# First layers of 18 groups of experts' tokens by seven products of half blocks, with weight sums made on GpSimd

## The chip, the core and the metric

The kernel runs on one core of a Trainium2 chip. The metric is the device time of one launch in microseconds: the median of three runs before is 1558.56 us (1558.34 to 1558.69). A core has five engines that matter here, each with a queue of its own that it works off strictly in order: PE (matrix products; PEld is its loading of weights), DVE (elementwise work, reads PSUM and SBUF), ACT (activations and copies, reads PSUM and SBUF), POOL (GpSimd: elementwise work on SBUF, and the indirect DMAs) and SP (which issues the other DMAs). Engines wait for each other through semaphores. [...]

## What is computed

One layer: a graph aggregation over a 4096 x 4096 matrix, an attention block, and a mixture of eight experts, of which each token takes two. The change is in the experts. All is float32.

```python
for e in range(NE):                       # NE = 8, HID = 682, C = 256
    hh = jax.nn.silu(flat @ w1[e].T) * (flat @ w3[e].T)
    out = out + weights[:, e:e + 1] * (hh @ w2[e].T)
return x + out.reshape(Bx, Tx, Cx)
```

`flat @ w1.T` and `flat @ w3.T` are the first layers, `hh @ w2.T` the second.

## The kernel before

The graph and the attention take the first 1043 us. Then the tokens, sorted by expert into `lists` in DRAM, are worked off in groups of one expert each: whole groups of 256 tokens and small groups of 128. `TURNS` lists them in order; k is the place in it, 0 to 41. Places 0 to 8 are whole, 9 to 36 mix 11 whole ones (10, 12, 15, 17, 20, 22, 25, 28, 30, 33, 35) with 17 small ones, 37 to 41 are whole. Nothing is rescheduled by a planner: each engine gets its instructions in the order in which the Python code issues them, and semaphores are put between.

For each k the loop runs, in this order: `hidden(k)`, the first layers with the activation, ending with the transposes and scaling of the next group's tokens (`prepare(k + 1)`: transposes `tx` on PE, two scalings L1383 on ACT); `load13(k + 5)`, the weights of both first layers; `combine(k - 1)`, the second layer of the group before, its weighting by the router, and an indirect DMA that adds each half of 128 tokens into DRAM (L1548 on POOL, after a short memset of `gap`); then `load_rows(k + 4)` and `load2(k + 4)`. Five buffers each hold w13, w2 and rows, `w13s[k % 5]` and so on.

`hidden` of a whole group: the hidden units are five blocks of 128 (`NF = 5`) and a rest of 42 units, whose w1 and w3 columns share one block. For each of these 11 blocks and both halves of C, one product of 128 x 128 weights with 128 x 256 tokens (L1476). They go to PSUM tiles of one or two banks from three pools (`p_sc0`, `p_sc1`, `p_sc2`, six banks together, shared with the attention's scores and accumulators `y_first` and `y_second`). ACT takes silu (L1482), DVE multiplies by the other product into `hT` (L1483).

Second layers of the 19 whole groups in `SEVEN` (k = 4 to 39) are already done in seven products of half blocks (Strassen's scheme in Winograd's form): `split(k)` makes four sums of quarters of hT and four of w2 on DVE (L1412 to L1419), `seven_products` does seven products of three blocks each (L1440), with 128 tokens or channels to a product, into two banks (`ye_y`, `ye_ms`), and adds them up with one copy on ACT (L1447) and seven adds on DVE (L1448 to L1454). ACT then weights both halves into y (L1539).

Of the kernel before, what the change touches and what calls it, by code (L numbers as in the profile page):

```python
# [9 lines left out]
F32 = mybir.dt.float32  # L10
# [5 lines left out]
PSUM = bass.MemoryType.PSUM  # L16
# [49 lines left out]
def fast_kernel(  # L66
# [596 lines left out]
    with (  # L663
# [1 line left out]
        tc.tile_pool(name="eg", bufs=1) as eg,  # L665
        tc.tile_pool(name="ex", bufs=2) as ex,
        tc.tile_pool(name="ax", bufs=2) as ax,
        tc.tile_pool(name="a_sc0", bufs=1, space=PSUM) as p_sc0,
        tc.tile_pool(name="a_sc1", bufs=2, space=PSUM) as p_sc1,
        tc.tile_pool(name="a_sc2", bufs=1, space=PSUM) as p_sc2,  # L670
        tc.tile_pool(name="a_y", bufs=1, space=PSUM) as p_y,
        tc.tile_pool(name="a_ms", bufs=1, space=PSUM) as p_ms,
    ):

        HALF = GR // P
        pt_all = sp.tile([P, 9 * 1024], F32, name="pt_all")
# [25 lines left out]
            given_back.update(keys)  # L702
            ring[:] = [r for r in ring if homes.get(id(r)) not in given_back]

        p_sc = cycle((p_sc0, p_sc2, p_sc1))
        p_sa = cycle((p_sc0, p_sc2))
        y_banks = [
            pool.tile([P, 512], F32, tag=tag, name=name) for pool, tag, name in (
# [681 lines left out]


        SEVEN = [k for k in range(4, NM - 2) if TURNS[k] < NW]
        parts_of = {}

        def split(k, hT):


            w2_sb = w2s[k % 5]
            m = {}
            for c in range(2):  # L1400
                chunks = hT.rearrange("p (j c) i -> p c j i", c=2)[:, c]
                weights = w2_sb.rearrange("p (j c) o -> p c j o", c=2)[:, c]
                for h in range(2):
                    m[f"A{h + 1}{c + 1}"] = chunks[:, :, h * P : (h + 1) * P]
                    m[f"G{c + 1}{h + 1}"] = weights[:, :, h * P : (h + 1) * P]
            first = k % 2 * 3
            for n, s in enumerate(("S1", "S2", "S4")):
                m[s] = kT[first + n][:, 0 : 3 * P].rearrange("p (j i) -> p j i", j=3)
            for n, s in enumerate(("T1", "T2", "T4")):
                m[s] = vv[first + n][:, 0:3, :]  # L1410
            m["S3"], m["T3"] = m["A21"], m["G12"]
            nc.vector.tensor_add(m["S1"], m["A21"], m["A22"])  # L1412
            nc.vector.tensor_sub(m["S2"], m["S1"], m["A11"])
            nc.vector.tensor_sub(m["S4"], m["A12"], m["S2"])
            nc.vector.tensor_sub(m["S3"], m["A11"], m["A21"])
            nc.vector.tensor_sub(m["T1"], m["G12"], m["G11"])
            nc.vector.tensor_sub(m["T3"], m["G22"], m["G12"])
            nc.vector.tensor_sub(m["T2"], m["G22"], m["T1"])
            nc.vector.tensor_sub(m["T4"], m["T2"], m["G21"])  # L1419
            parts_of[k] = m  # L1420
# [36 lines left out]
        def hidden(k, step=None, behind=None):  # L1457
# [4 lines left out]
            free_bank = k >= SEVEN[0]  # L1462

            for q in range(0, NF + 1, 2):
                pool = next(p_sc)
                if pool is p_sc1:
                    ps = [
                        pool.tile([P, 2, GR], F32, tag="sc", name=f"h_{i}_{q}_{m}")[:, :, 0:n]
                        for m in range(2)
                    ]  # L1470
                else:
                    ps = pool.tile([P, 2, 2, GR], F32, tag="sc", name=f"h_{i}_{q}")
                    ps = [ps[:, m, :, 0:n] for m in range(2)]
                for m in range(2 * q, min(2 * q + 4, 2 * NF + 1)):
                    for c in range(2):
                        nc.tensor.matmul(  # L1476
                            ps[m % 2][:, m // 2 - q, :], w13_sb[:, c, m * P : (m + 1) * P],
                            xT[:, c, :], start=(c == 0), stop=(c == 1),
                        )
                both = 2 if q + 1 < NF else 1  # L1480
                si = ax.tile([P, 2, n], F32, tag="rden", name=f"si_{i}_{q}")
                nc.scalar.activation(si[:, 0:both, :], ps[0][:, 0:both, :], AF.Silu)  # L1482
                nc.vector.tensor_mul(  # L1483
                    hT[:, q : q + both, :], si[:, 0:both, :], ps[1][:, 0:both, :]
                )
                if q == 0 and behind is not None and not free_bank:
                    prepare(behind)
                if step and q < NF - 1:
                    step()
# [4 lines left out]
            )  # L1494
            if behind is not None and free_bank:
                prepare(behind, p_ms, "ms")
            hidden_of[i] = hT
            if k in SEVEN:
                split(k, hT)
# [146 lines left out]
        def step():  # L1646
            for f in next(rest, []):
                f()

        load13(2)  # L1650
        load2(2)
        load13(3)
# [2 lines left out]
        for k in range(NM):  # L1655
            if k == NM - 1:


                between = iter([lambda: None, lambda: combine(k - 1)])
            hidden(  # L1660
                k, step if k < NM - 1 else lambda: next(between)(),
                k + 1 if k + 1 < NM else None,
            )
            step()
            if k + 5 < NM:
                load13(k + 5)
            if 0 < k < NM - 1:
                combine(k - 1)
                step()
            if k == NM - LAST:  # L1670
                nc.sync.dma_start(out, acc_dram[0:N, :])
            if k + 4 < NM:
                load_rows(k + 4)
            if k + 4 < NM:
                load2(k + 4)
        combine(NM - 1)
    kv_scope.close()
    return lists

# [736 lines left out]
```

## Time and profile before

The profile is one execution of 1558.78 us, of which the span from first to last instruction is 1557.0 us.

| | before |
|---|---|
| median of three runs | 1558.56 us |
| profiled execution, its span | 1558.78 us, 1557.0 us |
| PE busy | 1541.9 us |
| DVE, ACT, POOL busy | 1045.4, 488.1, 655.0 us |
| stretch of the experts 1100 to 1500 us: PE busy | 400.0 us of 400 |
| the same: DVE, ACT, POOL busy | 197.4, 103.6, 94.2 us |
| granted PE clock in that stretch | 1.00 |

How to read it: rows of the timeline give the start, the length, engine, line, operation, output and inputs of one instruction or of a merged run of equal ones, then in brackets how long the engine sat idle before it and what released it. In rows by form, the two numbers after the bar are the group's busy time in us and the mean of one in ns. Each float32 product shows as two records on PE, so the 22 products of a whole group's first layers are 44 rows.

### The profile page before, as it was taken

The numbers are of one execution on the slowest core, as the hardware profiler recorded it, in microseconds if no ns is written. First come the engines' busy times: TensorE is split into PE (matmuls) and PEld (weight loads), VectorE is DVE, ScalarE is ACT, GpSimd is POOL, SyncE is SP. The second block draws the span as 40 slices with busy tenths as digits, with TensorE's granted clock in tenths as the row PEclk, the third lists the DMA queues.
The fourth block names the chain that finished last, engine by engine and source line by source line (L and its number), as shares of the span: only waits on it lengthen the run. The fifth ranks groups of instructions, "written<-read, shape, count | busy, mean of one in ns | idle before, by whom it ended". The sixth has DMA issues, their size and how long they took to land.

```text
span 1557.0 us, 27444 instructions
## 1 busy us (share of the span) xinstructions
PE 1541.9 (99%) x10692; PEld 1133.8 (73%) x10692; DVE 1045.4 (67%) x2137; ACT 488.1 (31%) x884; POOL 655.0 (42%) x725
## 2 busy tenths in 40 slices
PE   8999999999999999999999999999999999999997
PEld 7888888888888643444444444358899999999996
DVE  7966677766766677779879878785565453544462
ACT  1101010010010356555665655652122222222221
POOL 3446557565565323364564553442422212122213
PEclk9999999999999999999999999999999999999999
DMA  6344444443444000011011011048677778777772
GB/s 236 129 129 146 139 139 135 139 139 136 139 136 142 32 1 16 29 36 51 29 57 33 29 39 37 22 184 314 192 229 207 228 249 264 232 242 246 237 232 29
DMA packets 68507, 209.34 MB, mean 134 GB/s; under 512 B 17488, under 2 KB 45520, under 8 KB 54736
## 3 DMA queue, kind: packets, MB, share of 16 engines
q1 hardware_dynamic: 55104, 189.50, 35.5%
q0 software_dynamic: 12720, 17.47, 5.8%
q8 instruction: 86, 1.41, 0.4%
q10 hardware_dynamic: 544, 0.52, 0.1%
q14 instruction: 53, 0.43, 0.1%
HBM read 184.48 MB, written 27.13 MB: 136 GB/s over the span
## 4 chain that ended last, share of the span: by engine, by line
PE 96%; DVE 2%; DMA 0%; POOL 0%; issue 0%; ACT 0%; SPq 0%; POOLq 0%; DVEq 0%; ACTq 0%
PE acc L493 25%; PE h L1476 21%; PE sc L757 14%; PE y_first L799 5%; PE y_second L799 5%; PE ye_y L1528 4%; PE y_third L799 4%; PE ye_y L1440 3%; PE ye_ms L1440 2%; PE pq L194 2%; PE ph L545 2%; PE pf L464 1%; PE po L876 1%; PE tx L1377 1%; PE trq L229 1%; PE tr L376 1%
## 5 line engine op out<-in xcount | busy, mean ns | idle before, releaser
L757 PE MATMUL sc<-qT_all,kT 64*64 64x512 f32 (+3 forms) x2304 | 282.0, 557 | 1.0 <-ACT pt_all L765 0.5
L493 PE MATMUL acc<-a,g 128*128 128x256 f32 x1024 | 245.9, 380 | 0.0
L1548 POOL DMA_INDIRECT acc_dram<-y,late x57 | 89.8, 1575 | 334.9 <-DVE y L1543 185.5
L493 PEld LDWEIGHTS acc<-a,g 128*128 128x128 f32 x1024 | 193.0, 190 | 31.6 <-DVE vv L511 1.2
L757 PEld LDWEIGHTS sc<-qT_all,kT 64*64 64x64 f32 x2304 | 91.2, 133 | 130.1 <-issue 108.2
L1483 DVE TENSOR_TENSOR late<-si,h 128x256 f32<-128x256 f32 (+2 forms) x126 | 62.7, 506 | 183.0 <-ACT si L1482 180.2
L765 ACT ACTIVATE pt_all<-sc 128x1024 f32<-128x1024 f32 (+3 forms) x157 | 149.0, 956 | 95.7 <-PE sc L757 95.1
L448 POOL TENSOR_TENSOR all_s<-all_s,more_sums 128x512 f32<-128x512 f32 x72 | 106.4, 1491 | 106.0 <-DVE more_sums L440 106.0
L1476 PE MATMUL h<-late,qT_all 128*128 128x256 f32 (+1 forms) x792 | 147.2, 345 | 0.0
L1482 ACT ACTIVATE si<-h 128x256 f32<-128x256 f32 (+2 forms) x126 | 57.0, 453 | 276.6 <-PE h L1476 269.4
L1476 PEld LDWEIGHTS h<-late,qT_all 128*128 128x128 f32 x792 | 130.1, 191 | 15.2 <-ACT late L1383 0.8
L493 PE MATMUL acc<-more_sums,g 128*128 128x256 f32 x512 | 126.2, 379 | 0.0
L785 DVE TENSOR_TENSOR late<-late,pt_all 128x1024 f32<-128x1024 f32 (+3 forms) x92 | 107.7, 1171 | 23.0 <-ACT pt_all L765 9.6
L1476 PE MATMUL h<-late,pt_all 128*128 128x128 f32 (+1 forms) x704 | 113.5, 321 | 0.0
L1476 PEld LDWEIGHTS h<-late,pt_all 128*128 128x128 f32 x704 | 103.5, 191 | 8.0
L493 PEld LDWEIGHTS acc<-more_sums,g 128*128 128x128 f32 x512 | 97.2, 190 | 14.8
L799 PE MATMUL y_second<-pt_all,vv 64*64 64x512 f32 (+3 forms) x440 | 105.0, 555 | 0.0
L799 PE MATMUL y_first<-pt_all,vv 64*64 64x512 f32 (+3 forms) x440 | 104.3, 553 | 0.0
L1035 POOL DMA_INDIRECT lists<-row,slots x64 | 90.2, 1410 | 18.0 <-issue 15.3
L799 PE MATMUL y_third<-pt_all,vv 64*64 64x512 f32 (+3 forms) x376 | 89.8, 557 | 0.0
L378 ACT COPY qT_all<-tr 128x512 f32<-128x512 f32 x30 | 16.2, 589 | 210.5 <-PE tr L376 210.4
L1476 PE MATMUL h<-late,res_all 128*128 128x256 f32 (+1 forms) x352 | 68.3, 353 | 0.0
(394 smaller groups left out, 2997.4 us busy)
## 6 DMA issues: line engine op xcount, KB each, us to landing
a<-in_adj_dram SPq DMA_DIRECT2D x64, 1024.0 KB
qT_all<-in_w_dram SPq DMA_DIRECT2D x18, 1408.0 KB
pt_all<-in_w_dram SPq DMA_DIRECT2D x16, 1408.0 KB
res_all<-in_w_dram SPq DMA_DIRECT2D x17, 768.0 KB
pt_all<-in_w_dram SPq DMA_DIRECT2D x16, 768.0 KB
res_all<-in_w_dram SPq DMA_DIRECT2D x8, 1408.0 KB
qT_all<-in_w_dram SPq DMA_DIRECT2D x9, 768.0 KB
late<-lists SPq DMA_DIRECT2D x25, 265.0 KB
```

Of the source, the lines that this page charges most:

```text
L448: nc.gpsimd.tensor_add(all_s[:, i], all_s[:, i], sums_at[n % 2][k])
L493: nc.tensor.matmul(acc[bank][:, at, :], g[jb][:, right, k, :], m[left][:, k, :], start=(jb == 0 and k == 0 and at == 0), stop=(jb == NB - ...
L757: nc.tensor.matmul(ps[k * HP : (k + 1) * HP, j, :w], kT[sb][hd, i * P + k * HP : i * P + (k + 1) * HP], qT[b][hd, p, off:], start=True, st ...
L765: nc.scalar.activation(pt[:, :, :w], ps[:, :, :w], AF.Exp, scale=HD ** -0.5)
L785: nc.vector.tensor_add(sums[b, p][:, :, off:], before[:, :, off:], pt[:, :, : 512 - off])
L799: nc.tensor.matmul(accs[b, p][k][hd, off:], vv[sb][some, i, hd], pt[some, j, : 512 - off], start=(s == order_of(b)[0]), stop=(s == order_o ...
L1035: put = nc.gpsimd.indirect_dma_start(out=lists[:, :], out_offset=bass.IndirectOffsetOnAxis(ap=chosen[b][:, k, t, :], axis=0), in_=flats[b] ...
L1440: nc.tensor.matmul(p[number], m[left][:, j, :], m[right][:, j, :], start=(n % 4 == 0 and j == 0), stop=(j == 2), skip_group_check=True,)
L1476: nc.tensor.matmul(ps[m % 2][:, m // 2 - q, :], w13_sb[:, c, m * P : (m + 1) * P], xT[:, c, :], start=(c == 0), stop=(c == 1),)
L1483: nc.vector.tensor_mul(hT[:, q : q + both, :], si[:, 0:both, :], ps[1][:, 0:both, :])
L1528: nc.tensor.matmul(ps[h if last else 0][:, h, :], hT[:, q, cols], w2_sb[:, q, :], start=(q == 0), stop=(q == NF),)
L1548: put = nc.gpsimd.indirect_dma_start(out=(acc_dram if k < NM - LAST else out)[:, :], out_offset=at, in_=y[:, h, :], in_offset=None, comput ...
```

## The change

The 18 groups `SPLIT13 = SEVEN[1:]` (k = 5, 6, 7, 8, the 11 mixed ones, 37, 38, 39) get their first layers in seven products for eight. With A the weights (rows: w1 or w3; columns: half of C) and B the tokens (rows: half of C; columns: half of the 256 tokens), the sums of weights are S1 = A21 + A22, S2 = S1 - A11, S4 = A12 - S2, S3 = A11 - A21, each 128 x 640, and of tokens T1 to T4, each 128 x 128. Each of the seven products is done for five blocks of 128 units with 128 tokens. The 42 remaining units keep their two products with 256 tokens.

- `sums13(k)` makes S1 to S4 on GpSimd; the loop calls it with k + 2 after `hidden` of k and ahead of `combine(k - 1)`. S3 is written over A21.
- `sums2(k)` makes two of the second layer's weight sums (T1, T3, 128 x 384) on GpSimd, a group ahead after `combine(k - 1)`; `split` leaves these two out on DVE.
- `sums_x(k)` makes the four sums of tokens on DVE after the tokens are prepared.
- `hidden_seven(k)` replaces `hidden(k)`. Blocks 0 to 3 are part `one`, block 4 is part `two`; each part has three banks, A, D and B. Products are added up in a bank: ACT copies a bank's value out, PE then adds the next product on top.
- The three pools of scores are closed after the attention, and a new pool `e_h` of six single banks serves all first layers, those of `hidden` too.

```diff
+        def sums13(k):
...
+            nc.gpsimd.tensor_add(m["S1"], m["A21"], m["A22"])
+            nc.gpsimd.tensor_sub(m["S2"], m["S1"], m["A11"])
+            nc.gpsimd.tensor_sub(m["S4"], m["A12"], m["S2"])
+            nc.gpsimd.tensor_sub(m["S3"], m["A11"], m["A21"])
+        def sums_x(k):
...
+            nc.vector.tensor_sub(m["T1"], m["B12"], m["B11"])
+            nc.vector.tensor_sub(m["T2"], m["B22"], m["T1"])
+            nc.vector.tensor_sub(m["T3"], m["B22"], m["B12"])
+            nc.vector.tensor_sub(m["T4"], m["B21"], m["T2"])
+        def hidden_seven(k, step, behind):
...
+            def product(q, bank, left, right, first=False):
+                for n, c in enumerate(q.chunks):
+                    nc.tensor.matmul(
+                        bank[:, n, :], m[left][:, c, :], m[right],
+                        start=first and n == 0, stop=True, skip_group_check=True,
+                    )
+            def copied(dst, q, bank):
+                nc.scalar.copy(dst, bank[:, 0 : len(q.chunks), :])
+            def added(dst, q, bank):
+                nc.vector.tensor_add(dst, dst, bank[:, 0 : len(q.chunks), :])
+            def begun(q):
+                product(q, q.A, "A11", "B11", True)
+                copied(q.s1, q, q.A)
+                product(q, q.D, "S1", "T1", True)
+                copied(q.s5, q, q.D)
+                product(q, q.B, "A12", "B21", True)
+            def second(q):
+                product(q, q.A, "S2", "T2")
+                copied(q.u2, q, q.A)
+                product(q, q.D, "S4", "B22")
+            def joined(q):
+                added(q.s1, q, q.B)
+                added(q.u2, q, q.D)
+                nc.scalar.activation(q.pair, q.pair, AF.Silu)
+            def third(q):
+                product(q, q.A, "S3", "T3")
+                copied(q.u3, q, q.A)
+                nc.vector.tensor_add(q.u3, q.u3, q.s5)
+            def last(q):
+                product(q, q.A, "A22", "T4")
+                nc.vector.tensor_mul(hT[:, q.rows, P:GR], q.u2, q.u3)
+                nc.vector.tensor_mul(
+                    hT[:, q.rows, 0:P], q.s1, q.A[:, 0 : len(q.chunks), :]
+                )
+            begun(one)
+            second(one)
+            joined(one)
+            step()
+            begun(two)
+            tail = two.B[:, 2:4, :].rearrange("p k i -> p (k i)")
+            for c in range(2):
+                nc.tensor.matmul(
+                    tail, w13_sb[:, c, 2 * NF * P :], xT[:, c, :],
+                    start=False, stop=(c == 1), skip_group_check=True,
+                )
+            third(one)
+            second(two)
+            joined(two)
+            si = ax.tile([P, GR], F32, tag="rden", name=f"si_{i}_t")
+            nc.scalar.activation(si[T0 : T0 + TAIL, :], tail[0:TAIL, :], AF.Silu)
+            nc.vector.tensor_mul(
+                hT[T0 : T0 + TAIL, NF, :], si[T0 : T0 + TAIL, :], tail[T0 : T0 + TAIL, :]
+            )
+            step()
+            if behind is not None:
+                prepare(behind, p_ms, "ms")
+            third(two)
+            last(one)
+            last(two)
+            if behind is not None:
+                sums_x(behind)
+            hidden_of[i] = hT
+            split(k, hT)
+        def sums2(k):
...
+            nc.gpsimd.tensor_sub(m["T1"], m["G12"], m["G11"])
+            nc.gpsimd.tensor_sub(m["T3"], m["G22"], m["G12"])
...
+        sc_scope.close()
+        p_h.append(ctx_h.enter_context(tc.tile_pool(name="e_h", bufs=6, space=PSUM)))
...
+            if k in SPLIT13:
+                hidden_seven(k, step, k + 1)
+            else:
+                hidden(
...
             step()
+            sums13(k + 2)
             if k + 5 < NM:
                 load13(k + 5)
             if 0 < k < NM - 1:
                 combine(k - 1)
                 step()
+            sums2(k + 1)
```

## The prediction

> **What bounds the kernel now.** First the page: busy times and the chain that ended last.
>
> ```profile
> PE 1541.9 (99%) x10692; PEld 1133.8 (73%) x10692; DVE 1045.4 (67%) x2137; ACT 488.1 (31%) x884; POOL 655.0 (42%) x725
> PE 96%; DVE 2%; DMA 0%; POOL 0%; issue 0%; ACT 0%; SPq 0%; POOLq 0%; DVEq 0%; ACTq 0%
> ```
>
> PE sets the end, so a product saved is time saved, as long as PE goes on without a gap. Then the timeline of two whole groups, k = 6 and 7, for what the other engines do beside it.
>
> ```profile
> 1134.01 9.66 PE L1476 MATMUL h<-late,qT_all 128*128 128x256 f32 x44
> ...
> 1143.50 0.60 PE L1377 MATMUL tx<-ident,late 128*128 128x128 f32 x4
> ...
> 1143.94 1.50 PE L1440 MATMUL ye_y<-qT_all,late 128*128 128x128 f32 x12
> ...
> 1145.03 0.56 DVE L1412 TENSOR_TENSOR kT<-late 128x384 f32<-128x384 f32 x1
> ...
> 1148.63 9.66 PE L1476 MATMUL h<-late,res_all 128*128 128x256 f32 x44
> 1148.94 0.56 DVE L1419 TENSOR_TENSOR vv<-vv,res_all 128x384 f32<-128x384 f32 x1
> ...
> 1151.49 1.03 ACT L1539 ACTIVATE y<-vv,gt 128x256 f32<-128x256 f32 x2 [4.41 <-DVE vv L1452]
> ...
> 1152.42 0.58 ACT L1482 ACTIVATE si<-h 128x512 f32<-128x512 f32 x1
> ```
>
> A group takes 14.62 us on PE (1134.01 to 1148.63): first layers 9.49, transposes 0.44, second layer 4.69. ACT's weighting of y for the group two places back ends at 1152.52, 3.9 us into the next first layers, and ACT's first silu starts behind it: ACT and DVE are already that late, and it costs nothing because six banks let PE run on. One 256-token record takes 9.49 / 44 = 0.2157 us; small groups give the 128-token record, (1467.01 - 1462.10) / 44 = 0.1116.
>
> **PE's gain.** 20 products of 256 tokens become 35 of 128, two records each: 40 x 0.2157 = 8.63 becomes 70 x 0.1116 = 7.81. That is 0.82 a group, 14.8 over 18 groups. The 42 remaining units keep four records, 0.86.
>
> **What is added on the path.** ACT and DVE now stand between two products in one bank. I walk through `hidden_seven`, us from its first product, with these rows: ACT copy of 128x512 0.589, of 128x128 0.266 (L1447), silu of 128x1024 as the 1024-wide exponential, of 128x256 0.384, of the tail 0.376 (L1491), a small group's scaling 0.364, a whole one's 0.471 (L1383); DVE 128x512 0.687 (L1483), 128x384 0.558, 128x128 0.288; 0.03 to 0.05 between releaser and next, a product's last record ending 0.28 after its start.
>
> ```profile
> L378 ACT COPY qT_all<-tr 128x512 f32<-128x512 f32 x30 | 16.2, 589 | 210.5 <-PE tr L376 210.4
> L765 ACT ACTIVATE pt_all<-sc 128x1024 f32<-128x1024 f32 x130 | 132.2, 1024 | 90.2 <-PE sc L757 90.0
> ```
>
> Five products of part one end at 4.46 on PE without a wait: the copies of s1 and s5 end at 1.7 and 2.7. Part two's first three run to 5.13, the tail to 5.99, `third(one)` to 6.88. ACT copies u3 from 7.10 to 7.69, DVE adds s5 until 8.42, then s1 and u2 of part two until 9.06; only then silu of part two to 9.48, the tail's silu 9.88, the next group's two scalings 10.65 (10.85 if it is whole), and then the copy of u3 of part two, 10.94 (11.14). PE meanwhile did the transposes and `last(one)` by 9.2 and stands before `last(two)`, which adds to the bank that this copy reads. It starts about 0.15 after the copy (the trace has no clean row for PE woken by ACT; bounds 0.03, the ACT to DVE step, and 0.3, from ACT L1383's end at 1043.37 to PE's start at 1043.67) and ends at 11.31 (11.51), against 9.71 (9.93) for the old block with its transposes. Everything queued on PE, the second layer first, waits with it. So each group loses 1.6 in place of gaining 0.82.
>
> The 11 mixed groups: a small group follows, 2.6 + 4.9 + 0.4 us on PE in which DVE finishes the multiplications (13.2) and the six remaining sums of `split` (16.6), needed at about 19. No more is lost: 11 x 1.6 = 17.6.
>
> In k = 5 to 8 and 37 to 39 whole group follows whole group, and a loop through ACT closes: the weighting of y is ahead of the next group's copy of s1 on ACT's queue, it waits for the seven adds, and these stand on DVE behind everything above. Counted from the start of copying s1: s1 done 0.59, S2 product 0.75, u2 copied 2.45, DVE 3.44, silu 4.50, two short copies 5.10, u3 copied 5.76, DVE 7.13, silu and tail 7.95, scalings 8.92, copy 9.21, DVE's add and four multiplications 11.62, token sums 4 x 0.32 = 12.9, six sums of split 16.3, router's two 16.7, seven adds and y 2.7 (1149.82 to 1152.52): 19.4. PE's own part of that is under 14, so 19.4 replaces 14.62.
>
> First stretch: s1 of k = 5 at 1.1, of k = 8 at 1.1 + 3 x 19.4 = 59.3; its last product ends at 68.7, then 4.7 + 5.4 + 4.7 for the second layers of 7 and 8 round the small group: 83.5 until k = 10 starts, where before it was 1187.71 - 1119.38 = 68.3: +15.2. Last stretch: k = 37 11.5, second layer of 36 2.6; in k = 38 DVE comes 1.0 late from the split of 37, and s1 starts at 15.2; of k = 39 at 15.2 + 1.0 + 19.4 = 35.6, its end at 45.0, second layer 49.7, before 1513.91 - 1472.13 = 41.8: +7.9.
>
> **The new pool.** In the order of the changed program the very first product of k = 0 waits for DVE's last add from `y_second`, since the closed pools give their banks back together; before, it took a bank that was free.
>
> ```profile
> 1043.67 3.72 PE L1476 MATMUL h<-late,qT_all 128*128 128x256 f32 x16
> ...
> 1045.80 0.68 DVE L808 TENSOR_TENSOR yT<-yT,y_second 128x512 f32<-128x512 f32 x1
> ```
>
> From 1043.67 to 1046.48 and 0.2 more: +3.0, with nothing else for PE to do.
>
> **GpSimd.** A 640-wide sum lies between the shortest 512 (1.257, L448) and 1024 wide ones (2.165, L892), about 1.5; four of them and two of 0.83 (L214, 384 wide) are 7.7 a group, beside 4.5 for two indirect DMAs with memsets. That fits into 16 to 20 us, and each is needed a group later, so the queue costs nothing; without the group's lead, S1 alone would hold PE 1.5. But they meet DVE.
>
> ```profile
> 917.58 1.23 DVE L785 TENSOR_TENSOR late<-late,res_all 128x1024 f32<-128x1024 f32 x1 [0.36 <-ACT res_all L765]
> 918.39 2.46 POOL L892 TENSOR_TENSOR res_all<-res_all,row 128x1024 f32<-128x1024 f32 x1
> 919.35 2.58 DVE L785 TENSOR_TENSOR late<-late,qT_all 128x1024 f32<-128x1024 f32 x1 [0.55 <-ACT qT_all L765]
> ```
>
> The same DVE add takes 1.35 longer beside a GpSimd add. Around 202 to 214 us seven 512-wide DVE adds beside GpSimd sums of about 1.05 took 1.03 on average, the median free one 0.684 (L441): +0.35, or 0.5 for sums of 1.5. On the path I count 18 such meetings: three in each of four cycles of 19.4, and the add of s5 in six mixed groups whose `sums13` starts near 7. I take 0.5, the nearer rows: 9; ends 0.25 (L438's mean, 0.929) and 1.35, so 4 to 24. [...]
>
> **Sum.** 3.0 + 15.2 + 17.6 + 7.9 + 9 = 52.7, PE's saving already inside. The profiled span of 1557.0 becomes 1609.7; the execution was 1.8 longer than its span and lies 0.2 from the median, so 1558.56 + 52.7 = 1611.
>
> **Rivals.** *Products decide* (faster): the chain behind `third(one)` hides and only the count matters: 1558.6 - 14.8 + 3.0 = 1547. For it speaks that PE never idles here now. It decides from the point where the last copy ends by 9.1, 1.8 earlier than walked; the queues are in order and each length is a measured row, so 0.06. *Stall without the loop*: each group loses its 1.6 but ACT and DVE don't run late from group to group: 18 x 1.6 + 3.0 = 31.8, 1590; for it, ACT is only 26% and DVE 49% busy here; 0.16. *GpSimd blocks fully*: meetings at 1.35: 43.7 + 24.3 = 68, 1627, and above where it reaches more of split's sums; 0.12. *Gains and stalls cancel*, or the change does less than it says: within 3 us of 1558.6; 0.03.
>
> **Numbers.** The forecast has 0.63. The range 1587 to 1631 takes in the stall alone and the full blocking. About 0.2% (3 us) is what a measurement can tell from no change: faster 0.06, same 0.02, slower 0.92.
>
> **What would show it.** In the changed profile: PE idle before the last products of part two, released by ACT's 128x128 copy, about 1.8 us in each of 18 groups; blocks of 11 to 12 us for mixed groups; 19 to 22 us from k = 6 to 7 and 7 to 8 with PE waiting for the copy of s1 behind y; 3 us idle near 1044; DVE's 384-wide sums longer than 0.56 where GpSimd is busy. I am wrong if PE shows no idle time there, or if the whole groups in a row keep below 16 us.

## The result and the profile after

The changed kernel takes 1633.03 us, the median of six runs (1630.85 to 1633.38); the kernel before took 1558.45 on the same chip. The ratio is 1.0476, 95% interval 1.0463 to 1.049: 74.6 us slower. The forecast was 1611 with a range up to 1631, so the direction was right and the size too small, by 22 us and 2 us beyond the range.

The page of the profiled execution (1633.38 us, its span 1631.7) first, busy times and the chain that ended last:

```profile
PE 1558.5 (96%) x11232; PEld 1158.3 (71%) x11232; DVE 1129.7 (69%) x2299; ACT 538.0 (33%) x1010; POOL 805.6 (49%) x833
PE 88%; DVE 5%; ACT 3%; issue 2%; POOL 1%; DMA 0%; SPq 0%; DVEq 0%; POOLq 0%; ACTq 0%
```

PE's share of the span fell from 99 to 96%, and DVE, ACT and "issue" now hold a tenth of the chain. PE is also busy 16.6 us longer than before, although the products should have saved it 14.8.

The timeline of PE and ACT at the start of the experts and in the groups k = 5 and 6 shows the waits that the prediction named, and one that it didn't:

```profile
1047.06 3.72 PE L1642 MATMUL h<-late,qT_all 128*128 128x256 f32 x16 [2.80 <-DVE yT L809]
...
1138.59 0.80 PE L1478 MATMUL hA<-kT,res_all 128*128 128x128 f32 x2 [6.87 <-ACT hz L1484]
...
1154.63 1.03 ACT L1707 ACTIVATE y<-vv,gt 128x256 f32<-128x256 f32 x2 [5.58 <-DVE vv L1623]
1155.57 0.57 ACT L1484 COPY wqkv_sb<-hA 128x512 f32<-128x512 f32 x1
...
1156.23 1.13 PE L1478 MATMUL hA<-kT,sum_all 128*128 128x128 f32 x8 [2.80 <-issue]
```

The first row is the new pool: 2.80 us idle until DVE's add. The last three are the loop through ACT: y, the copy of s1 right behind it, and PE's second product into that bank, which starts 0.1 us after the copy's end. The 6.87 us in k = 5 were not foreseen. No stop ends with one of GpSimd's sums: of PE's 25 idle times over 0.3 us from 1120 us on, 24 end 0.05 to 0.10 us after an ACT copy and one behind a token sum of DVE.

In a mixed group (k = 10, then k = 12) the timeline of PE, DVE, ACT and POOL shows this:

```profile
1229.40 1.58 POOL L1417 TENSOR_TENSOR sum_all<-res_all 128x640 f32<-128x640 f32 x1
1230.00 1.53 DVE L1509 TENSOR_TENSOR hy<-hy 128x512 f32<-128x512 f32 x1 [2.29 <-ACT hy L1484]
...
1231.96 0.42 ACT L1504 ACTIVATE hz<-hz 128x256 f32<-128x256 f32 x1 [1.83 <-DVE hz L1487]
...
1232.81 0.63 ACT L1384 ACTIVATE late<-tx,ln_sb 128x128 f32<-128x128 f32 x2
1233.32 0.27 ACT L1484 COPY hz<-hA 128x128 f32<-128x128 f32 x1
...
1233.64 0.80 PE L1478 MATMUL hA<-kT,qT_all 128*128 128x128 f32 x2 [2.07 <-ACT hz L1484]
1234.23 4.00 PE L1696 MATMUL ye_y<-pt_all,late 128*128 128x256 f32 x12
...
1258.61 0.49 PE L1478 MATMUL hA<-kT,res_all 128*128 128x128 f32 x2 [1.23 <-ACT hz L1484]
1258.93 2.76 PE L1696 MATMUL ye_y<-res_all,late 128*128 128x256 f32 x12
```

PE stops before the last product of part two and goes on with the 128x128 copy of u3, as walked. In k = 12 the stop is 1.23 us; in k = 10 DVE's add of s5 started beside a GpSimd sum, took 1.53 instead of 0.69, and the stop became 2.07. Then something else: the same twelve products of the second layer take 4.00 us behind the longer stop and 2.76 behind the shorter.

Timeline of DVE and POOL at the last stretch, k = 37:

```profile
1527.82 2.12 POOL L1417 TENSOR_TENSOR sum_all<-pt_all 128x640 f32<-128x640 f32 x1
1528.03 2.06 DVE L1433 TENSOR_TENSOR kT<-late 128x128 f32<-128x128 f32 x1 [0.18 <-ACT late L1384]
1530.01 1.54 POOL L1418 TENSOR_TENSOR sum_all<-sum_all,pt_all 128x640 f32<-128x640 f32 x1
1530.19 1.50 DVE L1434 TENSOR_TENSOR kT<-late,kT 128x128 f32<-128x128 f32 x1
...
1533.28 1.58 POOL L1420 TENSOR_TENSOR pt_all<-pt_all 128x640 f32<-128x640 f32 x1
1533.39 1.50 DVE L1676 TENSOR_TENSOR pick<-late,mine 128x16 f32<-128x16 f32 x1
```

Two token sums of 0.28 and 0.29 us alone last 2.06 and 1.50 us here, beside GpSimd sums of 2.12 and 1.54, and a 16-wide multiplication of 0.17 lasts 1.50 beside one of 1.58. y of k = 36 stands behind them, and PE then waits 4.21 us for the copy of s1.

By stretch (starts of the groups' first products in the two profiles, us; the right column is the first experiment):

| | before | walked | after | sums left out |
|---|---|---|---|---|
| up to k = 5 | 1119.4 | +3.0 | +3.4 | +5.3 |
| k = 5 to 10 | 68.3 | +15.2 | +31.2 | +15.0 |
| k = 10 to 37, mixed | 284.4 | +17.6 | +24.7 | +12.3 |
| k = 37 to the end | 84.9 | +7.9 | +15.4 | +7.0 |
| sum | 1557.0 | +43.7, and 9 for GpSimd | +74.7 | +39.6 |

PE's part of this (its idle time, and its busy time for the same 11232 products, in the two right-hand profiles):

| | idle after | idle, sums left out | busy after | busy, sums left out |
|---|---|---|---|---|
| up to k = 5 | 9.8 | 9.1 | 1113.0 | 1115.7 |
| k = 5 to 10 | 22.6 | 14.0 | 76.9 | 69.3 |
| k = 10 to 37, mixed | 20.7 | 15.4 | 288.4 | 281.3 |
| k = 37 to the end | 20.1 | 14.6 | 80.2 | 77.3 |
| sum | 73.2 | 53.0 | 1558.5 | 1543.6 |

### The profile page after: what moved, and what is told of

Same layout as the page of the kernel before. It is cut to its first block, busy times and chain, and to the rows that moved or that the text cites. A ratio compares the mean times of both kernels' runs of the same rounds, so it can differ in the third digit from the quotient of the medians.

```text
span 1631.7 us, 29131 instructions
## 1 busy us (share of the span) xinstructions
PE 1558.5 (96%) x11232; PEld 1158.3 (71%) x11232; DVE 1129.7 (69%) x2299; ACT 538.0 (33%) x1010; POOL 805.6 (49%) x833
## 4 chain that ended last, share of the span: by engine, by line
PE 88%; DVE 5%; ACT 3%; issue 2%; POOL 1%; DMA 0%; SPq 0%; DVEq 0%; POOLq 0%; ACTq 0%
PE acc L493 23%; PE sc L758 13%; PE h L1642 9%; PE ye_y L1696 4%; PE y_second L800 4%; PE y_third L800 4%; PE y_first L800 4%; PE hA L1478 4%; PE ye_y L1611 3%; PE pq L194 2%; PE ye_ms L1611 2%; PE hD L1478 2%; PE ph L545 2%; PE pf L464 1%; DVE sum_all L786 1%
## 5 line engine op out<-in xcount | busy, mean ns | idle before, releaser
L493 PEld LDWEIGHTS acc<-more_sums,g 128*128 128x128 f32 x512 | 97.2, 190 | 14.8
L1648 ACT ACTIVATE si<-h 128x256 f32<-128x256 f32 (+2 forms) x72 | 28.7, 398 | 166.1 <-PE h L1642 158.6
L1649 DVE TENSOR_TENSOR late<-si,h 128x256 f32<-128x256 f32 (+2 forms) x72 | 31.4, 439 | 69.4 <-ACT si L1648 38.8
L768 POOL TENSOR_SCALAR_AFFINE_SELECT pt_all<-pt_all 128x256 f32<-128x256 f32 x36 | 20.4, 569 | 107.5 <-ACT pt_all L766 79.8
L1642 PE MATMUL h<-late,qT_all 128*128 128x128 f32 (+1 forms) x440 | 70.0, 317 | 2.8 <-DVE yT L809 2.8
L1642 PEld LDWEIGHTS h<-late,qT_all 128*128 128x128 f32 x440 | 63.6, 191 | 9.2 <-DVE yT L809 3.7
L493 PE MATMUL acc<-qT_all,g 128*128 128x256 f32 x256 | 65.7, 379 | 0.0
L1642 PE MATMUL h<-late,pt_all 128*128 128x128 f32 (+1 forms) x484 | 65.2, 294 | 0.0
```

Source lines behind the costliest of these rows:

```text
L493: nc.tensor.matmul(acc[bank][:, at, :], g[jb][:, right, k, :], m[left][:, k, :], start=(jb == 0 and k == 0 and at == 0), stop=(jb == NB - ...
L1642: nc.tensor.matmul(ps[m % 2][:, m // 2 - q, :], w13_sb[:, c, m * P : (m + 1) * P], xT[:, c, :], start=(c == 0), stop=(c == 1),)
```

## The experiments

All times are medians; the kernel before ran beside each set at 1558.4 to 1558.6.

**What GpSimd's sums cost.** The six sums of weights are left out, so the split groups compute with weights that were not summed; nothing else changes.

```diff
-            nc.gpsimd.tensor_add(m["S1"], m["A21"], m["A22"])
...
-            nc.gpsimd.tensor_sub(m["T3"], m["G22"], m["G12"])
```

> The six sums on GpSimd per group are left out (first and second layers of the 18 groups then work on stale sums, so part of the computation is missing); PE, ACT and DVE keep every instruction. If the chain of copies on ACT and the loop through DVE are the main cause and GpSimd only adds to it: the mixed groups that had a stall of 2.1 to 2.3 us before their last product fall to the 1.23 of the others, DVE's add of s5 returns from 1.5 to 0.69 us, and the time is near 1600 (1592 to 1608), still 34 to 50 above before. If GpSimd's exclusion of DVE is the whole cause: below 1570. If it is no cause: 1633.

1598.28 (1596.54 to 1598.39), ratio 1.0251 [1.0233, 1.0268]: the sums are worth 34.7 of the 74.6 us. Rows by form of DVE, first in the changed kernel (busy us, mean ns), then without the sums:

```profile
L1509 DVE TENSOR_TENSOR hy<-hy 128x512 f32<-128x512 f32 x18 | 21.9, 1215 | 42.4 <-ACT hy L1484 42.4
L1513 DVE TENSOR_TENSOR late<-qT_all,hy 128x512 f32<-128x512 f32 x9 | 10.2, 1130 | 0.0
L1487 DVE TENSOR_TENSOR qT_all<-qT_all,hB 128x512 f32<-128x512 f32 x9 | 6.2, 686 | 13.2 <-PE hB L1478 10.0 <-ACT qT_all L1484 3.1
```

```profile
L1505 DVE TENSOR_TENSOR hy<-hy 128x512 f32<-128x512 f32 x18 | 12.5, 692 | 41.4 <-ACT hy L1480 36.2 <-ACT hz L1480 2.7 <-issue 2.5
L1509 DVE TENSOR_TENSOR late<-qT_all,hy 128x512 f32<-128x512 f32 x9 | 6.2, 685 | 0.0
```

The add of s5 (both inputs in SBUF) has a mean of 1215 ns with the sums and 692 without, the multiplication of `qT_all` and `hy` 1130 and 685. The add of `hB`, whose second input lies in PSUM, has a mean of 686 with the sums too, and the add of `hD` at 1158.36, with an input in PSUM as well, took 0.69 us beside a GpSimd sum that ran from 1158.31 for 1.58. Over the whole run the same 2299 DVE instructions are busy 1129.7 us with the sums and 1091.7 without, 38.0 more. From 1120 us on, 36 rows of DVE's timeline are more than 0.2 us over the shortest row of their line and form; together they are 34.5 over, 0.96 each. The rows are not all on the path: between k = 10 and 37 they are 19.8 us longer, and PE's idle time there grows by 5.3. Of the 35.1 us between the two spans, 20.2 are idle time of PE and 14.9 are PE taking longer over the same products; the next experiment shows why. What is left without the sums, 39.6 of span, is close to the walk without its term for GpSimd, 43.7.

A TENSOR_SCALAR of 128x8 took 1.53 us beside a GpSimd sum of 1.54, and 0.16 without the sums. Timeline of POOL and DVE just ahead of k = 5, first in the changed kernel, then DVE without the sums:

```profile
1120.49 1.54 POOL L1418 TENSOR_TENSOR sum_all<-sum_all,qT_all 128x640 f32<-128x640 f32 x1
1120.53 1.53 DVE L1288 TENSOR_SCALAR ends<-ends 128x8 f32<-128x8 f32 x1
```

```profile
1120.48 0.16 DVE L1288 TENSOR_SCALAR ends<-ends 128x8 f32<-128x8 f32 x1
```

**What the stops do to PE's rate.** Ten transposes that nobody reads keep PE busy in part of each stop before the last product of part two.

```diff
             last(one)
+            for n in range(10):
+                nc.tensor.transpose(one.B[:, n % 4, :], ident, ident)
             last(two)
```

> The changed kernel with ten transposes of the identity into part one's third bank, whose sums have long been read, put on PE ahead of the last product of part two: about 10 x 0.11 = 1.1 us of PE work that nobody reads, inside a stall of 1.23 to 2.3 us. Theory (half rate follows a stall of 2 us or more, none follows one of 1.23): the five mixed groups that show a stall of 2.1 to 2.3 us keep full rate behind it and save some 1.2 us each, and two or three of the groups in a row as much: 1623 to 1629, the 12 matmuls behind the wait of k=10 at 2.8 us instead of 4.0. Rival (the rate is halved for another reason, such as power or a schedule of its own): 1632 to 1637, and the 12 matmuls stay at 4.0.

1626.66 (1625.42 to 1631.49), ratio 1.0448 [1.0431, 1.0465]; 6.4 us less, with more work on PE. Timeline of PE, k = 10:

```profile
1230.80 1.25 PE L1543 MATMUL hB<-ident 128*128 128x128 f32 x10
1233.03 0.49 PE L1478 MATMUL hA<-kT,qT_all 128*128 128x128 f32 x2 [0.98 <-ACT hz L1484]
1233.36 2.76 PE L1698 MATMUL ye_y<-pt_all,late 128*128 128x256 f32 x12
```

The last product starts no earlier against its group (11.35 us after the first, 11.36 in the changed kernel), but the second layer behind it is back at 2.76. In the changed kernel eight second layers from k = 5 on begin at about half rate, some 1.2 to 1.7 us too long each, 11.6 together, and the granted clock from 1120 to 1220 us is 0.88; in this run no second layer does. Parts of first layers run at half rate too, in k = 5, 8 and 37 of the changed kernel (granted clock 0.50 from 1134.34, 1195.78 and 1537.11 us on).

The half rate is the granted clock, and the trace of the changed kernel tells when it fell. In the stretch of the experts it is either 1.00 or 0.50 there, and each of its 20 stretches from 1134.34 to 1625.86 us lasts 3.41 us or a whole multiple of that (the first two 13.65 and 17.07). Such windows around the last product of k = 15, then around the second product of k = 6 (length; busy time of PE, PEld, DVE, ACT, POOL; granted clock; DMA share, GB/s):

```profile
1287.94:1291.35 3.41, 1.08 (x9) 0.89 (x8) 2.14 (x5) 1.57 (x5) 3.33 (x3) 1.00 0.70 262
1291.35:1294.77 3.42, 3.42 (x10) 2.71 (x9) 3.25 (x7) 0.00 (x0) 0.38 (x2) 0.50 0.75 222
...
1151.41:1154.82 3.41, 2.02 (x19) 1.83 (x17) 3.11 (x11) 0.19 (x1) 0.00 (x0) 1.00 0.06 23
1154.82:1158.23 3.41, 2.00 (x18) 2.03 (x19) 0.98 (x2) 2.37 (x5) 2.62 (x3) 1.00 0.21 15
1158.23:1161.65 3.42, 3.42 (x28) 3.12 (x27) 1.00 (x2) 2.13 (x5) 3.34 (x4) 1.00 0.73 112
```

In k = 15 the whole stop of 2.33 us lies in one window, and the next window has a clock of 0.50. The longer stop of k = 6, 2.80 us, is spread over two windows with about 1.4 us idle in each, and the clock stays at 1.00. From 20 us on, eleven windows of this trace at 1.00 are followed by one at 0.50, and in each of the eleven PE was idle for 1.92 to 2.92 us; in none that is followed by another at 1.00 was it idle for more than 1.76. In the kernel before, the window from 1547.03 us with 1.88 us idle is followed by one at 1.00, and that one, idle throughout, by one at 0.50. With the ten transposes the stop of k = 10 is 0.98 us; its window in the changed kernel had 1.94 us idle, and the next ran at 0.50.

In windows at 0.50 PE is busy 41.0 us in the changed kernel. The granted clock over the span is 0.984 there (1631.7 us) and 0.995 without the sums (1596.6 us), which makes 26.1 and 8.0 us lost by the estimate (1 - clock) x span, with windows in which PE was idle among them: 18.1 apart, where PE's busy times differ by 14.9. The +5.3 before k = 5 in the table fits that: without the sums PE is busy 2.7 us longer there (1115.7 against 1113.0), and in the run with only the mixed groups, below, the sixteen product rows behind the same wait of 2.80 us for the new pool took 5.41 us for 3.72. That the run without the sums lost its time there too is an estimate.

**ACT's order.** Part two's third product, and with it the copy of u3, goes ahead of its silu, the tail's and the scalings.

```diff
             second(two)
+            third(two)
             joined(two)
...
-            third(two)
             last(one)
```

> Only the order changes: the third product of part two and the copy of its u3 come ahead of the two silus of part two, the tail and the scalings on ACT. If the place of that copy on ACT's queue makes the stall before the last product: the stall (1.23, or 2.1 to 2.5 where GpSimd blocks) vanishes in all 18 groups, with the slow records of PE after the long ones, and the time falls by 20 to 32, to 1601 to 1613. If DVE's work as a whole sets the pace and the stall only moves: within 5 of 1633.

1627.54 (1624.78 to 1629.03), ratio 1.0445 [1.0428, 1.0462]: a miss, only 5.5 us. Timeline of PE, k = 10:

```profile
1231.09 0.49 PE L1478 MATMUL hA<-kT,qT_all 128*128 128x128 f32 x2 [0.40 <-ACT hz L1484]
...
1232.75 2.76 PE L1696 MATMUL ye_y<-pt_all,late 128*128 128x256 f32 x12
...
1243.17 2.22 PE L1611 MATMUL ye_y<-qT_all,late 128*128 128x128 f32 x12 [2.32 <-DVE y L1711]
```

The first layers take 9.56 us (1223.19 to 1232.75), below the 9.72 of before. But the time comes back ten us later: PE waits 2.32 us for y of the small group, which stands on DVE behind the eight sums of `split`, and twelve products behind that wait take 2.22 us for 1.60. In the groups in a row the waits for s1 grow from 2.80, 2.37, 1.92 to 4.67, 4.28, 3.12. A stop on PE had been hiding DVE's lateness.

**y on DVE.** The weighting of y for the split groups is taken from ACT.

```diff
-                    nc.scalar.activation(
-                        y[:, h, :], done[h].rearrange("p h o -> p (h o)"), AF.Copy, scale=gt[:, h]
+                    nc.vector.tensor_scalar(
+                        y[:, h, :], done[h].rearrange("p h o -> p (h o)"), gt[:, h], None,
```

> The weighting of y of the groups in SEVEN goes from ACT to DVE (two of 0.48 us there in place of two of 0.51 on ACT). If the loop through ACT's queue (y ahead of the next copy of s1) costs the whole groups in a row: their stalls before the second product in bank A (2.80, 2.37, 1.92, 4.21, 1.93 us in k = 6, 7, 8, 37, 39) shrink, and the time falls by 4 to 12, to 1621 to 1629. If DVE by itself bounds these stretches: no faster, 1630 to 1640.

1622.71 (1622.02 to 1626.98), ratio 1.042 [1.0402, 1.0437], as the loop through ACT's queue would have it. The waits of 2.80 and 2.37 for s1 are gone; waits of 2.60 and 2.71 before the last products of k = 6 and 7 stand in their place.

**The new pool.** The banks of the scores are kept for k = 0 to 4 and given back at k = 5.

```diff
-        sc_scope.close()
...
         for k in range(NM):
+            if k == SPLIT13[0]:
+                sc_scope.close()
```

> The score pools stay open for the first layers of k = 0 to 4 and are closed before k = 5. If giving the banks back together costs the 2.8 us before the first product of the experts: that gap closes and the time falls by 2.8 (2 to 4), to about 1630. If the wait comes back at k = 5 or is hidden anyway: within 1 of 1633.

1631.02 (1627.2 to 1634.66), ratio 1.0456 [1.0438, 1.0473]. The 2.80 us at the start are gone, and k = 5 waits 3.69 us for its banks instead: no gain that can be told from the spread.

**Which groups.** Only the mixed groups are split, and then all but the first of the row.

```diff
-        SPLIT13 = SEVEN[1:]
+        SPLIT13 = [k for k in SEVEN if ALONE < k < NM - LAST]
```

> Only the eleven whole groups between smaller ones are split (k=10 to 35); the whole groups in a row at the start (k=5 to 8) and at the end (k=37 to 39) go as before. Theory (the losses by stretch as the changed kernel's trace has them: start of the experts 3.4, first stretch 31.2, mixed 24.7, last 15.4): 1558.6 + 3.4 + 24.7 = 1587, between 1581 and 1592. Rival (losses are carried from one stretch into the next, so that the mixed groups do better or worse without the first stretch ahead of them): under 1579 or over 1595. The prediction's walk for the same groups: 3.0 + 17.6 + 5.5 = 1585, which this run can't tell from the theory; but by the walk the other two stretches were worth 23 of the loss and not 46.6, so 1633 less this run is the better measure of them: 46 by the trace, 27 by the walk with its GpSimd share.

1586.72 (1585.4 to 1589.17), ratio 1.0179 [1.0162, 1.0196]. As the table by stretch says: the seven groups in a row cost 1633.0 - 1586.7 = 46.3, the eleven mixed ones and the start 28.

```diff
-        SPLIT13 = SEVEN[1:]
+        SPLIT13 = SEVEN[2:]
```

> The changed kernel with the split begun at k=6, so that k=5 goes as before. Theory (k=5 is dear for its own reason: the table's last step of 4.3 us and the eight sums of k=4 stand on DVE ahead of it, and GpSimd's sums hold the small operations): k=5 to k=6 falls from 27.8 us to about 14.6, and k=6, now first of the row, has no y ahead of its first copy: 1633 - 13 - 2 = 1618, between 1612 and 1622. Rival (what made k=5 slow waits for the first split group wherever it is): k=6 takes over the 6.9 us stall, 1624 to 1630. The prediction's walk gave k=5 no more than 2 us and the loop 4.8: 1626.

1629.66 (1626.27 to 1636.58), ratio 1.0449 [1.0432, 1.0467]: the theory fell, and the rival's range holds the result. Timeline of PE in the longest of the four executions, k = 6, now the first of the row:

```profile
1154.38 2.04 PE L1478 MATMUL hA<-kT,sum_all 128*128 128x128 f32 x8 [9.59 <-issue]
```

Its stop is longer than the one it replaces. What made k = 5 slow isn't the table's step alone; here too the first split group waits for a copy of s1, which ends 0.1 us before PE goes on and stands on ACT behind y, and y waits for DVE, which had the eight sums of the group before and GpSimd's sums beside them.

**DVE's order.** In the changed kernel the eight sums of `split` go behind the sums that make y of the group before.

```diff
-            split(k, hT)
...
                 combine(k - 1)
+                if k in SEVEN:
+                    split(k, hidden_of[TURNS[k]])
                 step()
```

> The changed kernel with only this edit: the eight sums of a group's second layer go on DVE behind the sums that make y of the group before. Theory (the loop of the groups in a row, and the long stall of its first group, run through these eight sums: 4.5 us alone, 6 to 8 where GpSimd holds them): the loop falls by about 4.5 us a group, in seven groups in a row about 20 to 28 us: 1605 to 1613, and the stall of k=5 falls from 6.9 us to under 3. Rival (ACT's order and GpSimd's hold bind, and DVE's order doesn't): 1628 to 1636.

1649.15 (1648.51 to 1649.53), ratio 1.058 [1.0564, 1.0597]; the worst of all. By stretch it goes both ways: k = 5 to 10 takes 92.3 us instead of 99.5, no product waits for s1 in k = 6 to 8 any more, and from k = 37 on it is 6.1 shorter; but the mixed stretch takes 338.4 instead of 309.1. So the loop does run through these sums, as walked, and where a small group comes next they are needed early. k = 5 in the timeline of PE, DVE and POOL:

```profile
1134.48 2.40 DVE L1586 TENSOR_TENSOR pt_all<-pt_all 128x384 f32<-128x384 f32 x1
1134.89 1.58 POOL L1559 TENSOR_TENSOR vv<-qT_all 128x384 f32<-128x384 f32 x1
...
1138.19 1.77 DVE L1589 TENSOR_TENSOR vv<-vv,pt_all 128x384 f32<-128x384 f32 x1
...
1142.45 0.80 PE L1478 MATMUL hA<-kT,res_all 128*128 128x128 f32 x2 [10.74 <-ACT hz L1484]
```

The sums that were moved now start beside GpSimd's, and 0.56 us become 1.77 and 2.40.

**A better order.** Both parts' copies first on ACT, then the third and last products, then silus and scalings; with all 18 groups, then with the eleven mixed ones.

```diff
             begun(one)
             second(one)
-            joined(one)
-            step()
             begun(two)
+            third(one)
+            second(two)
...
+            joined(one)
+            third(two)
+            last_product(one)
+            last_product(two)
+            joined(two)
+            step()
```

> All 18 groups, in another order of issue: both parts' first five products and their four or five copies come first on ACT, then the third and last products of both, then the silus, scalings and multiplications; so no product waits for a copy that stands behind a silu. Theory (in groups in a row the pace is a loop PE, DVE, ACT, y, next group's first copy, and the multiplications now come later in it; in mixed groups the stall of 1.23 goes, while GpSimd's sums still hold DVE): first and last stretch as bad as before or some us worse, mixed groups 1 to 1.5 us each better: 1633 - 15 + 4 = 1622, between 1612 and 1632. Rival (the order of copies was all that held it): the stalls go everywhere, 1560 to 1595.

> The same order of issue, and only the eleven mixed groups split. Theory: the run with the eleven groups in the old order (1587 expected) less 11 x 1 to 1.5 us = 1573, between 1565 and 1580. Rival one (the stall only moves to the second layer, as it did with the third product put ahead: -5.5 over all groups): 1581 to 1587. Rival two (without PE stalls each group saves its full 1.06 us against the old first layer): 1558.6 + 3.4 - 11 x 1.06 = 1550, faster than the kernel before.

All 18: 1637.36 (1634.8 to 1638.3), ratio 1.0501 [1.0483, 1.0518], outside what was expected; k = 6 waits 6.17 us for its s1. Mixed only: 1584.41 (1583.54 to 1587.09), ratio 1.0165 [1.0148, 1.0182]: the last product still waits 1.35 us or more for u3, whose copy stands behind part one's silu. So that silu went behind the copy too, and the score banks were kept until k = 10:

```diff
-            joined(one)
...
             last_product(two)
+            silu(one)
             joined(two)
+            silu(two)
```

> The run with the eleven mixed groups in the new order of issue (1584.4), with two more edits: part one's silu goes behind the copy of part two's third product on ACT (there PE waited 1.35 us or more for that copy in the groups from k=10 to 25), and the banks of the scores are kept until k=10. Theory: the stall of 1.35 goes in all eleven groups, some 11 to 15 us, and up to 3 us at the start of the experts: 1567 to 1571. Rival one (the stall moves to the second layer, because DVE is late with hT): 1577 to 1584. Rival two (the banks' release brings a wait at k=10 instead): as the theory, 3 us more.

1573.29 (1571.02 to 1575.49), ratio 1.01 [1.0083, 1.0116], the expectation missed by 2 us. k = 10 starts 4.1 us earlier than in the run before (1189.53 against 1193.61), so the pool's term is real where its banks come back in time; 1.4 of the 4.1 is the rate of the sixteen rows behind the pool's 2.80 us, which took 5.13 us in the run before and 3.72 here. The first layers now have no stop, and a block takes 8.90 us (k = 10, 1189.53 to 1198.43) against 9.72 before: the 0.82 of the prediction. PE waits only for y of the small group, in the timeline:

```profile
1208.58 1.60 PE L1630 MATMUL ye_y<-qT_all,late 128*128 128x128 f32 x12 [2.05 <-DVE y L1737]
```

From k = 10 to 35 such waits, with two short ones for ACT's scalings, add up to 15.3 us, more than the 11 x 0.82 = 9.0 that the products save. Four experiments on this version tried to take them away.

```diff
-            nc.gpsimd.tensor_add(m["S1"], m["A21"], m["A22"])
+            nc.vector.tensor_add(m["S1"], m["A21"], m["A22"])
```

(and so for the other five sums)

> The same, with the six sums of weights of each split group on DVE instead of GpSimd (by the 0.56 us of a 384-wide sum there, 4 x 0.86 + 2 x 0.56 = 4.6 us of DVE per group, where DVE is idle for 45% of the stretch). Theory (GpSimd's sums cost by shutting DVE out, not by the work itself): no DVE sum takes more than its own time, no second layer waits for DVE, and each group saves the 0.55 us that its 7/8 of the products leave: 1552 to 1560, same as the kernel before or a little faster. Rival (4.6 us more on DVE's queue hold up the scalings and y behind them, and PE waits for DVE): 1565 to 1590.

1585.12 (1584.23 to 1586.43), ratio 1.0174 [1.0157, 1.019]: the rival. Waits for y grow to 3.5 us, since the sums now stand ahead of it.

`split` behind y, as above:

> The eleven mixed groups in the new order (1573.3), with the eight sums of a group's second layer put on DVE behind the sums that make y of the group before, not ahead of them. Theory (what is left of the loss there, 15.3 us of PE waiting for y of a smaller group, is y's place behind the eight sums on DVE, 8 x 0.56 us and more where GpSimd holds them): most of it goes, 1558 to 1563, about level with the kernel before, since each group saves only 0.55 us of products. Rival (GpSimd's own hold on DVE makes y late, whatever stands ahead): 1568 to 1575.

1586.28 (1584.72 to 1587.23), ratio 1.0177 [1.0163, 1.0191]: neither. The waits for y are gone and waits of 2.56 to 2.86 for the sums of `split` are there, which now run into GpSimd's.

y of the smaller groups on ACT, its weights made before the next first layers; with the sums on GpSimd and on DVE:

```diff
+            if SPLIT13[0] <= k <= NM - LAST:
+                gate(k - 1)
...
+                elif SPLIT13[0] - 1 <= k < NM - LAST:
+                    nc.scalar.activation(
+                        y[:, h, :], ps[0][:, h, :], AF.Copy, scale=gt[:, h]
+                    )
```

> The eleven mixed groups in the new order (1573.3), and y of the smaller groups among them weighted on ACT instead of DVE, with its weights (pick and its sum) computed on DVE before the next group's first layer and not behind its eight sums. Theory (the 15.3 us that second layers waited there for y of the smaller group are y's place in DVE's queue): they go, and 1558 to 1562 is left, level with the kernel before. Rival (GpSimd's hold makes the next thing on DVE late, hT or the sums made from it): 1565 to 1573.

> The same with the six sums of weights on DVE. Theory (DVE has the room of 4.6 us a group, and only y's place behind them cost the 26.7 us of the run with y on DVE, whose waits for y of 3.5 us are gone here): 1554 to 1562. Rival (4.6 us more ahead of the scalings or the eight sums make those late): 1566 to 1580.

With the sums on GpSimd 1591.53 (1590.09 to 1593.59), ratio 1.0212 [1.0198, 1.0226]; on DVE 1569.32 (1567.72 to 1571.33), ratio 1.0071 [1.0057, 1.0085], the best of all split versions, though in the rival's range and not the theory's. The first was to gain 12 us and lost 18. Its timeline of DVE, POOL and PE shows why:

```profile
1224.27 1.56 POOL L1757 DMA_INDIRECT acc_dram<-y,late  x1 [5.26 <-ACT y L1748]
1224.92 2.90 DVE L1600 TENSOR_TENSOR kT<-late 128x384 f32<-128x384 f32 x1
1225.29 2.11 POOL L1426 TENSOR_TENSOR res_all<-qT_all 128x640 f32<-128x640 f32 x1
...
1227.48 1.74 POOL L1427 TENSOR_TENSOR res_all<-res_all,qT_all 128x640 f32<-128x640 f32 x1
1227.86 1.78 DVE L1601 TENSOR_TENSOR kT<-kT,late 128x384 f32<-128x384 f32 x1
...
1233.30 2.50 PE L1630 MATMUL ye_y<-res_all,late 128*128 128x128 f32 x10 [4.47 <-DVE late L1603]
```

GpSimd's 640-wide sums stand behind the indirect DMA of y (1224.27, then 1225.29). y came earlier, so the sums came earlier too, straight beside the eight sums of `split`, and the first four of those, 0.56 us alone, each took 1.77 us or more. The 22 us between the two runs are what six sums a group cost on GpSimd rather than on DVE in that place, the clock (0.990 against 0.997 over the span) behind the stops of 4.3 to 4.5 us included. With the sums on DVE, PE waits 2.03 to 2.16 us in five groups for ACT's scaling of the next tokens. That stands behind a silu which waits for DVE, and DVE is making the sums of weights. Timeline of ACT and PE, behind k = 10:

```profile
1210.49 0.28 ACT L1674 ACTIVATE si<-h 128x128 f32<-128x128 f32 x1 [5.03 <-DVE late L1675]
...
1211.98 0.94 PE L1630 MATMUL ye_ms<-vv,kT 128*128 128x128 f32 x6 [2.03 <-ACT late L1390]
```

No version beats the kernel before. The 9.0 us are there, and no order that was tried freed DVE enough to keep them.

## Why the prediction was wrong, point by point

- *PE's gain, 0.82 a group:* right, as the best order shows where nothing stops PE (8.90 against 9.72).
- *Start, 3.0:* right. 2.80 us idle are in the trace, 3.4 with what lies before.
- *First stretch without GpSimd, 15.2:* 15.0 with the sums left out. The sum is right, its parts less so: the loop takes 17.9 us between the starts of k = 6, 7 and 8 where 19.4 were walked, and k = 5 takes 19.7 to the start of k = 6, with a stop of 3.72 that the walk didn't have.
- *Mixed groups, 17.6:* 12.3 without the sums. The stop is 1.23 us and the block 10.83 (k = 12) where 11.31 was walked. Part of it is that ACT's rows overlap: the scalings of 0.63 start at 1232.81 in k = 10 and the copy behind them at 1233.32, where the walk laid each after the end of the last.
- *Last stretch, 7.9:* 7.0 without the sums.
- *GpSimd, 9 with ends 4 and 24:* this is the step that failed. The sums cost 34.7 where 9 was written. By the two profiles, 35.1 apart, 20.2 is waiting and 14.9 is PE taking longer over the same products, at a granted clock of 0.984 against 0.995. The waiting is the term as it was meant, and it was mis-sized: 20.2 for 9. "I take 0.5" became 0.82 to 1.12 where the add of s5 met a sum in a mixed group (1.51 to 1.81 us for 0.69); the six such groups that were counted were five. In the groups in a row the count left out what isn't on the path by the walk but stands ahead of it in DVE's queue: the multiplications that read two SBUF tiles (L1513, up to 2.03 us for 0.68), the token sums (up to 2.06 for 0.28), even the weights of y (1.50 for 0.17). The size came from rows of GpSimd sums of 1.05 us that met DVE by chance; here sums of 1.5 to 2.1 us follow each other with at most 0.1 between them, and in k = 37 three token sums (at 1528.03, 1530.19 and 1531.82) each met one and took 2.06, 1.50 and 1.65 us. The row at 919 of the kernel before, 1.35 longer, was nearer to that. That 36 lengthened rows of 0.96 make 34.5 is no check on the 34.7: not all of them hold up PE, and the clock is in no row of DVE.
- *The clock behind a stop, in no term:* the sum charged a stop with its length and nothing more. That left out the 14.9; filling stops with transposes gave back 6.4, net of what the transposes themselves took. In the mixed groups it is the larger part of what GpSimd's sums cost: 7.1 of 12.4.
- *Rival "GpSimd blocks fully", 1627:* the nearest, and still low by 6, partly by luck. Its 1.35 a meeting was above the mean of 0.96, its 18 meetings too few, and it had nothing for the clock.
- *What would show it:* the stops before part two's last products, the y ahead of s1 and the 3 us near 1044 were all there, but the stops were 1.23 to 2.56 us and not 1.8 each, and from k = 7 to 8 it took 18.3 us, below the 19 to 22 that were named (21.3 from 6 to 7). DVE's 384-wide sums were not longer in the changed kernel's mixed groups: they ran while GpSimd waited for y. They were as soon as y came earlier.

What stays open is how the 6.87 us of k = 5 divide between the table's step, the eight sums and y on DVE; without GpSimd's sums 3.72 of it remain, and the run that begins at k = 6 shows only that the table's step isn't needed for such a stop.

## What to carry to other kernels

Before work is given to an idle GpSimd, list every DVE instruction in the stretch whose inputs all lie in SBUF, not just those on the critical chain: in the changed kernel 36 of them took 0.44 to 1.77 us longer beside GpSimd's sums than the shortest of their form, and the TENSOR_SCALAR of 128x8 above 1.53 us for 0.16. Any that stands in DVE's queue ahead of what PE waits for can delay it, as the eight sums of `split` delayed y, for which PE waited 2.32 us behind k = 10 with the third product put ahead. A stop of PE can cost more than its length: in the changed kernel eleven windows of 3.41 us in which PE was idle for 1.92 us or more were each followed by one at a granted clock of 0.50. Where a new dependency makes two in-order queues meet in a loop, taking away one wait mostly uncovers the next: here the stop before the third copy became a wait for y (2.32 us), that one a wait for the eight sums (2.56 to 2.86), and that one a meeting with GpSimd (1.77 us or more for 0.56). And a split of a product pays only while PE runs on without a stop: a stop of 1.23 us before the last product, the shortest in the changed kernel's mixed groups, already costs more than the 0.82 saved.

## What the hardware did that was not expected

- Behind stops of PE of 2.07 to 2.56 us, twelve products took 2.7 instead of 1.50 us or 4.0 to 4.4 instead of 2.76. The length of the stop alone didn't tell: one of 2.04 us in k = 35 lay across two windows with 0.82 and 1.41 us idle, the clock stayed at 1.00, and the twelve products took 2.75; behind waits of 2.05 to 2.47 for y in the mixed groups' new order twelve products took 1.60, as behind the short waits there.
- A DVE instruction on 16 elements a partition took 1.50 us beside a GpSimd sum of 1.58, for 0.17 alone, and the 128x512 add of s5 in k = 10 took 1.53 beside one of 1.58, for 0.69 alone: in these two the length went by GpSimd's instruction and not by DVE's own.
